# Flamingo layers on one core: the second pass's attention output by two levels of seven block products

## The chip, the cores and the metric

The kernel runs on one core of a Trainium2 chip. The metric is device time in microseconds (us) of one execution; the time before is the median of three runs. The program is static: every engine (TensorE, VectorE, ScalarE, GpSimd, and SyncE, which issues nearly all transfers) executes its own list of instructions in order, and semaphores tie the lists together. A profile of one execution lies beside the times.

## The reference

Two layers act on x, 8 sequences of 256 rows of 1024 numbers in float32. Layer 0 adds a gated autocorrelation attention (FFT, top 11 lags, softmax) and a gated linear layer with low-rank parts. Layer 1, which the change concerns, adds gated cross attention over a context and a gated linear layer:

```
x = x + tanh(g_xattn[0]) * autocorrelation(layernorm(x), ctx)
x = x + tanh(g_ffn[0])   * (W h + b + one of four low-rank parts)
q = rope(h @ wq)   # 32 heads of 128; k = rope(ctx @ wk), v = ctx @ wv: 8 heads each
w = softmax(where(mask, q k^T / sqrt(128), -1e9))
x = x + tanh(g_xattn[1]) * (concat_heads(w v) @ wo)       # wo: 4096 x 1024
x = x + tanh(g_ffn[1])   * (W1' h + b1)                   # fourier part folded into W1'
```

h is the layernorm of x at that point. All products are in float32.

## The kernel before, in words

Rows go through in two passes (p = 0, 1) of four sequences, eight tiles of 128 rows each. A pass has four stages: autocorrelation with the keys and values of the pass beside it (keys_values), lora_ffn, attention, fourier_ffn. Keys and values go to DRAM and come back by head group.

Large matrix products are done as seven block products in place of eight. Of A B with both cut into 2 x 2 blocks, left_operands makes four combinations of A's blocks, right_operands four of B's, and the results of the products 1, 2, 6, 7, 4, 5, 3 (SEVEN) are combined by combine (L220, into a fresh tile) or add_product (L252, straight into x, scaled by the gate): partial sums named u and w are carried along. Combinations of weights are made once, stored in DRAM, and loaded in later blocks (load_wq L862, load_wo L884).

Attention has 16 steps a pass: two blocks of 512 rows times eight head groups. In a step, for each of four combinations (n: sequence, l: head half) the program issues scores (L969: four products, a memset by GpSimd, a masked copy and a maximum by VectorE, exp by ScalarE, two scalings by VectorE), then some of the next step's queries, then values of the combination before (L1006: transposes, ScalarE copies, products). The output products of the step before fill in between: outputs (L942), seven products by two row tiles, each of two matmuls of 128x512 into one PSUM bank. The lists q_fill and o_fill (L1046) say how many products are issued in each quarter; the last step's outputs come after the loop (L1089). Queries take seven products of eight matmuls of 128x256 (L929), and rope (L714) turns them: three VectorE products and one GpSimd add (L723). PSUM tiles of queries and outputs share four banks (ps_mm).

A scheduler puts the instructions of each engine in order when the program is built: it goes by program order as priority, takes what it holds ready first, and inserts semaphore waits and buffer reuse. So a transfer or a GpSimd operation that is ready early may stand well ahead of its place in the program. Buffers are pools with a number of slots per tag: weights of queries and outputs have seven slots of 512 KB each, and a load waits until TensorE has released its slot. All transfers but the scattered output rows are issued by SyncE in one list.

## Time and profile before

| | us |
|---|---|
| median of three runs | 3401.23 (3399.96 to 3401.61) |
| profiled execution | 3396.83 |
| its span, first to last instruction | 3395.0 |
| TensorE busy in the span | 3314.1 |
| VectorE | 2252.4 |
| GpSimd | 1354.6 |
| ScalarE | 859.7 |
| one attention step, in either pass | 65.65 |

Times in the table are of one profiled execution but for the first line. A row of the profile's groups reads: line of the kernel, engine, operation, tiles written and read, shapes, count, then busy time and mean nanoseconds of one, then the time the engine sat idle just ahead of them and what ended it. Matmuls overlap, so that the mean of one is longer than the distance between two.

### The profile page before, as it was taken

The page shows a single profiled execution, that of the slowest core. Times are in us where ns is not written, and L with a number is a line of the kernel's source. Part 1 is how long each engine was busy: PE and PEld are TensorE (multiplying, and loading weights), DVE is VectorE, ACT ScalarE, POOL GpSimd, SP SyncE. Part 2 cuts the span into 40 slices and gives each one's busy share as a digit, 9 for nine tenths or more (in the row PEclk, how much of TensorE's full clock was granted, in tenths as well). Part 3 has the DMA queues.
Part 4 walks back from the last instruction along what each step waited for, and adds up shares of the span by engine and source line. Part 5 has one row for each costly group of instructions (what it writes and reads, how often), then busy time and mean ns, then how long its engine had stood idle before and what let it go on. Part 6 is the DMA issues. An engine that isn't in the chain of part 4 may idle for free. (4 is left out here: it accounts for less than half of the span.)

```text
span 3395.0 us, 36926 instructions
## 1 busy us (share of the span) xinstructions
PE 3314.1 (98%) x12784; PEld 2279.1 (67%) x12784; DVE 2252.4 (66%) x4229; ACT 859.7 (25%) x2061; POOL 1354.6 (40%) x1213
## 2 busy tenths in 40 slices
PE   8899999999999999999999999999999999999999
PEld 6566546767767776775467766577767776776654
DVE  7787666877777666665657775556666666666563
ACT  1233111322222222222123321112222322222220
POOL 4665212344443443344335542123443444344332
PEclk9999999999999999999999999999999999999999
DMA  7433634333333333343153424053333333333411
GB/s 270 170 115 102 207 115 155 130 140 127 137 127 131 121 119 123 118 155 118 56 196 130 147 96 146 17 173 115 118 125 120 115 118 121 121 118 122 158 44 50
DMA packets 161864, 431.72 MB, mean 127 GB/s; under 512 B 21476, under 2 KB 56292, under 8 KB 161678
## 3 DMA queue, kind: packets, MB, share of 16 engines
q1 hardware_dynamic: 160526, 425.17, 36.3%
q0 software_dynamic: 1152, 4.19, 0.3%
q8 instruction: 102, 1.67, 0.2%
q14 instruction: 84, 0.69, 0.1%
HBM read 350.66 MB, written 78.64 MB: 126 GB/s over the span
## 5 line engine op out<-in xcount | busy, mean ns | idle before, releaser
L723 POOL TENSOR_TENSOR qT<-rope,rope 128x512 f32<-128x512 f32 x128 | 170.2, 1330 | 867.5 <-DVE rope L722 867.5
L958 PE MATMUL po<-wo,oT 128*128 128x512 f32 x960 | 432.1, 593 | 0.0
L929 PE MATMUL ps_q<-xn,wq 128*128 128x256 f32 x1920 | 428.9, 379 | 0.0
L375 DVE SCALAR_TENSOR_TENSOR x<-po,tg,x 128x512 f32<-128x512 f32 x376 | 269.1, 745 | 196.0 <-PE po L958 70.5
L929 PEld LDWEIGHTS ps_q<-xn,wq 128*128 128x128 f32 x1920 | 364.8, 190 | 50.5 <-PE po L682 0.5
L991 ACT ACTIVATE s<-s,nmx 128x256 f32<-128x256 f32 x512 | 256.0, 501 | 277.0 <-DVE nmx L988 276.5
L986 DVE COPY_PREDICATED s<-keep,ps_s 128x512 f32<-128x512 uint8 x256 | 185.9, 729 | 182.2 <-PE ps_s L977 177.7
L958 PEld LDWEIGHTS po<-wo,oT 128*128 128x128 f32 x960 | 177.4, 190 | 175.6 <-issue 170.5
L958 PE MATMUL po<-wo,oS 128*128 128x512 f32 x640 | 287.7, 592 | 0.3 <-DVE x L375 0.3
L929 PE MATMUL ps_q<-xn_t,wq 128*128 128x256 f32 x1280 | 285.6, 379 | 0.0
L1018 ACT COPY wT<-pt 128x512 f32<-128x512 f32 x256 | 138.1, 590 | 515.9 <-PE pt L1012 515.7
L929 PEld LDWEIGHTS ps_q<-xn_t,wq 128*128 128x128 f32 x1280 | 243.2, 190 | 33.1
L1023 PE MATMUL av<-wT,v 128*128 128x256 f32 x1024 | 246.2, 383 | 5.1 <-ACT wT L1018 5.1
L977 PE MATMUL ps_s<-kT,qT 128*128 128x256 f32 x1024 | 247.9, 379 | 0.0
L1023 PEld LDWEIGHTS av<-wT,v 128*128 128x128 f32 x1024 | 191.4, 190 | 80.0 <-issue 44.0
L1000 DVE TENSOR_SCALAR s<-s,tot 128x256 f32<-128x256 f32 x512 | 220.0, 470 | 7.7
L985 POOL MEMSET s<- 128x512 f32 x256 | 130.0, 527 | 220.7 <-PE pt L1012 219.0
L958 PEld LDWEIGHTS po<-wo,oS 128*128 128x128 f32 x640 | 118.9, 190 | 136.7 <-issue 128.9
L977 PEld LDWEIGHTS ps_s<-kT,qT 128*128 128x128 f32 x1024 | 191.6, 190 | 25.3 <-DVE x L375 0.5
L258 POOL TENSOR_TENSOR x<-x,part 128x512 f32<-128x512 f32 x80 | 109.1, 1364 | 229.5 <-ACT part L257 222.1
L988 DVE TENSOR_REDUCE nmx<-s 128x2 f32<-128x512 f32 x256 | 175.0, 685 | 8.3
L263 POOL TENSOR_TENSOR x<-x,part 128x512 f32<-128x512 f32 x80 | 104.7, 1310 | 172.7 <-DVE part L375 157.0
(257 smaller groups left out, 5594.0 us busy)
## 6 DMA issues: line engine op xcount, KB each, us to landing
wq<-in_wq_dram SPq DMA_DIRECT2D x104, 512.0 KB, 3.2
wo<-in_wo_dram SPq DMA_DIRECT2D x104, 512.0 KB, 3.2
wq<-wq_d SPq DMA_DIRECT2D x96, 512.0 KB, 3.2
wo<-wo_d SPq DMA_DIRECT2D x96, 512.0 KB, 3.2
w<-w_d SPq DMA_DIRECT2D x36, 512.0 KB, 4.8
wk<-in_wk_dram SPq DMA_DIRECT2D x26, 512.0 KB, 5.9
wv<-in_wv_dram SPq DMA_DIRECT2D x26, 512.0 KB, 3.8
wk<-wk_d SPq DMA_DIRECT2D x24, 512.0 KB, 4.5
```

The source lines that it names most:

```text
L375: nc.vector.scalar_tensor_tensor(xs, ps, g, xs, ALU.mult, ALU.add)
L723: nc.gpsimd.tensor_add(dst, t0, t1)
L929: nc.tensor.matmul(ps[:, l, :], wops[r][:, l, c, :], xo[r][:, c, :], start=(c == 0), stop=(c == KH - 1),)
L958: nc.tensor.matmul(po, ops[r][:, h, t * P : (t + 1) * P], wops[r][:, h, :], start=(h == 0), stop=(h == 1),)
L977: nc.tensor.matmul(ps[:, t, :], qT[i, n][:, l, t * P : (t + 1) * P], kT[:, n * S : (n + 1) * S], start=True, stop=True,)
L985: nc.gpsimd.memset(s, MASKED)
L986: nc.vector.copy_predicated(s, keep[b], ps)
L988: nc.vector.tensor_reduce(nmx, s, AX.X, ALU.max, negate=True)
L991: nc.scalar.activation(s[:, t, :], s[:, t, :], AF.Exp, bias=nmx[:, t : t + 1], accum_out=tot[:, t : t + 1],)
L1000: nc.vector.tensor_scalar(s[:, t, :], s[:, t, :], tot[:, t : t + 1], None, ALU.mult)
L1018: nc.scalar.copy(wT[i], pt)
L1023: nc.tensor.matmul(av[:, i, :], kv[step][1][:, n * 2 + c, :], wT[i][:, c, :], start=(c == 0), stop=(c == 1),)
```

## The change

In pass 2 (the last), outputs gives way to outputs_of_two. It waits for the attention outputs of two head groups (two steps) and treats the product of 512 rows, 1024 columns of heads and 1024 output columns as seven products of halves, each of which is again seven products of halves: 49 products, each of two matmuls of 128x256. The left operands of the first level are made in place by GpSimd, those of the second level by GpSimd a product ahead (finer); the second level's results are gathered in c from u, v and m, the first level's in x by further adds. The right operands (49 per pair of groups) are read from wo2_d, 256 KB each, two per transfer (stream_wo). They are made in pass 1 by finer_weights: 28 chunks, each with two loads, four GpSimd subtractions and seven stores, issued one per quarter from the second block on. Fill lists of pass 2 count single products. Outputs of a pair spread over the two steps that follow it; the last pair's come after the loop.

To make room, rope works in place with one temporary, keys and queries are combined straight into the tile that is stored or used, key and value loads have three buffers for four, attention outputs 13 for 8 in pass 2, and the keys' rope table is loaded in each pass into a tile of the first stage.

```diff
--- before.py
+++ after.py
...
-    tab = const.tile([P, 2, S], F32, name="tab")
     tab_q = const.tile([P, 2, S], F32, name="tab_q")
...
+    wo2_d = [dram.tile([P, 49, 2, S], F32, name=f"wo2_d{i}") for i in range(N_KV // 2)]
...
-    def rope(dst, ps, cos, sin, pool):
+    def rope(x, cos, sin, pool):
         H = P // 2
-        t0 = pool.tile([P, 2, S], F32, tag="rope0", name="rope0", bufs=1)
-        t1 = pool.tile([P, 2, S], F32, tag="rope1", name="rope1", bufs=1)
+        t = pool.tile([P, 2, S], F32, tag="rope", name="rope", bufs=1)
         tab = lambda t: t.unsqueeze(1).to_broadcast([t.shape[0], 2, S])
-        nc.vector.tensor_mul(t0, ps, tab(cos))
-        nc.vector.tensor_mul(t1[0:H], ps[H:P], tab(sin[H:P, :]))
-        nc.vector.tensor_mul(t1[H:P], ps[0:H], tab(sin[0:H, :]))
-        nc.gpsimd.tensor_add(dst, t0, t1)
-
-    def keys_values(n, groups, pools):
+        nc.vector.tensor_mul(t[0:H], x[H:P], tab(sin[H:P, :]))
+        nc.vector.tensor_mul(t[H:P], x[0:H], tab(sin[0:H, :]))
+        nc.vector.tensor_mul(x, x, tab(cos))
+        nc.gpsimd.tensor_add(x, x, t)
+    def keys_values(n, groups, pools, tab):
...
-                dest = (lambda: new("c")) if kind == "wk" else out_tile
-                done = combine(r, ps, tiles, new, dest)
+                done = combine(r, ps, tiles, new, out_tile)
...
-                        kT = out_tile()
-                        rope(kT, c, tab[:, 0, :], tab[:, 1, :], w1)
+                        rope(c, tab[:, 0, :], tab[:, 1, :], w1)
                         place = kT_d.rearrange("(q l i) p t -> q i p l t", l=2, i=2)
                         nc.sync.dma_start(
-                            place[i_u, i, :, :, t0 + j * S : t0 + (j + 1) * S], kT
+                            place[i_u, i, :, :, t0 + j * S : t0 + (j + 1) * S], c
...
-            xn = pool.tile([P, D], F32, tag="xn", name="xl")
+            xn = new()
...
+            def finer_weights():
+                for two in range(N_KV // 2):
+                    for n, r in enumerate(SEVEN):
+                        w = [
+                            w1.tile([P, 2, HALF], F32, tag=f"fine{k}", name=f"fine{k}")
+                            for k in range(2)
+                        ]
+                        for k in range(2):
+                            nc.sync.dma_start(w[k], wo_operand(two * 2 + k, r))
+                        q = [[w[k][:, :, j * S : (j + 1) * S] for j in range(2)] for k in range(2)]
+                        t = [
+                            w1.tile([P, 2, S], F32, tag=f"fine_t{i}", name=f"fine_t{i}")
+                            for i in (1, 2, 4)
+                        ]
+                        ops = right_operands(nc.gpsimd, q, *t)
+                        for i, r2 in enumerate(SEVEN):
+                            nc.sync.dma_start(wo2_d[two][:, n * 7 + i], ops[r2])
+                        yield
+            def stream_wo():
+                places = [
+                    wo2_d[g // 2][:, n : min(n + 2, 49)]
+                    for blk, g in steps[::2]
+                    for n in range(0, 49, 2)
+                ]
+                tiles = []
+                for n in range(len(places)):
+                    while len(tiles) < min(n + 6, len(places)):
+                        src = places[len(tiles)]
+                        tiles.append(big_tile(go, [2, 2, S], "wo"))
+                        nc.sync.dma_start(tiles[-1][:, 0 : src.shape[1]], src)
+                    for i in range(places[n].shape[1]):
+                        yield tiles[n][:, i]
...
-                kT = w2.tile([P, NB], F32, tag="kv", name="kT", bufs=4)
+                kT = w2.tile([P, NB], F32, tag="kv", name="kT", bufs=3)
-                v = w2.tile([P, NBT, DH], F32, tag="kv", name="v", bufs=4)
+                v = w2.tile([P, NBT, DH], F32, tag="kv", name="v", bufs=3)
...
-                    done = combine(r, ps, tiles, lambda tag: half(tag, 1), lambda: half("c", 2))
+                    done = combine(r, ps, tiles, lambda tag: half(tag, 1), lambda: half("qT", 7))
                     if done:
-                        qT[done[1]] = half("qT", 8)
-                        rope(qT[done[1]], done[0], tab_q[:, 0, :], tab_q[:, 1, :], w1)
+                        qT[done[1]] = done[0]
+                        rope(done[0], tab_q[:, 0, :], tab_q[:, 1, :], w1)
...
+            def outputs_of_two(blk, qs):
+                g, ng = tg_x[1], ntg_x[1]
...
+                s1 = [half("oT", 13) for _ in qs]
+                for q, s in zip(qs, s1):
+                    nc.gpsimd.tensor_add(s, q[1][0], q[1][1])
+                    nc.gpsimd.tensor_sub(q[1][0], q[0][0], q[1][0])
+                at = lambda i, k: [q[i][k] for q in qs]
+                ops = {1: at(0, 0), 2: at(0, 1), 6: at(0, 0), 7: at(1, 0), 4: at(1, 1), 5: s1}
+                ops[3] = ops[2]
...
+                def finer(r):
+                    q = [[o[:, :, t * P : (t + 1) * P] for o in ops[r]] for t in range(2)]
+                    made = {1: q[0][0], 2: q[0][1], 4: q[1][1]}
+                    def make():
+                        for i, (op, y, z) in {
+                            5: (nc.gpsimd.tensor_add, q[1][0], q[1][1]),
+                            7: (nc.gpsimd.tensor_sub, q[0][0], q[1][0]),
+                            6: (nc.gpsimd.tensor_sub, 5, q[0][0]),
+                            3: (nc.gpsimd.tensor_sub, q[0][1], 6),
+                        }.items():
+                            made[i] = w2.tile([P, 2, P], F32, tag="oI", name=f"oI{i}", bufs=5)
+                            op(made[i], *(made[v] if isinstance(v, int) else v for v in (y, z)))
+                            yield
+                    return made, make()
+                left, make = finer(SEVEN[0])
+                for _ in make:
+                    pass
+                part = None
+                for n, r in enumerate(SEVEN):
+                    g1, g2 = (ng, g) if r == 4 else (g, ng)
+                    c = [half("co", 6) for t in range(2)]
+                    for r2 in SEVEN:
+                        w = next(wo_stream)
+                        po = ps_mm.tile([P, S], F32, tag="mm", name="po")
+                        for h in range(2):
+                            nc.tensor.matmul(
+                                po, left[r2][:, h, :], w[:, h, :], start=(h == 0), stop=(h == 1)
+                            )
+                        scaled = nc.vector.scalar_tensor_tensor
+                        if r2 == 1:
+                            u = quarter("o_u", 1)
+                            nc.scalar.activation(u, po, AF.Copy, scale=g1)
+                        elif r2 == 2:
+                            scaled(c[0][:, 0, :], po, g1, u, ALU.mult, ALU.add)
+                        elif r2 == 6:
+                            scaled(u, po, g1, u, ALU.mult, ALU.add)
+                        elif r2 == 7:
+                            v = quarter("o_w", 1)
+                            scaled(v, po, g1, u, ALU.mult, ALU.add)
+                        elif r2 == 4:
+                            scaled(c[1][:, 0, :], po, g2, v, ALU.mult, ALU.add)
+                        elif r2 == 5:
+                            m = quarter("o_m", 1)
+                            nc.scalar.activation(m, po, AF.Copy, scale=g1)
+                            nc.gpsimd.tensor_add(u, u, m)
+                            nc.gpsimd.tensor_add(c[1][:, 1, :], v, m)
+                        elif r2 == 3:
+                            scaled(c[0][:, 1, :], po, g1, u, ALU.mult, ALU.add)
+                        if r2 in (2, 6, 7, 5):
+                            next(coming[1], None)
+                        if r2 != 3:
+                            yield
+                    for t in range(2):
+                        ct = c[t].rearrange("p b s -> p (b s)")
+                        add = lambda eng, y: eng.tensor_add(y, y, ct)
+                        if r == 1:
+                            add(nc.gpsimd, x[t][0][0])
+                        elif r == 2:
+                            add(nc.vector, x[t][0][0])
+                        elif r == 6:
+                            add(nc.vector, part[t])
+                            nc.gpsimd.tensor_add(x[t][0][1], x[t][0][1], part[t])
+                        elif r == 7:
+                            nc.vector.tensor_add(ct, ct, part[t])
+                            add(nc.gpsimd, x[t][1][0])
+                            add(nc.gpsimd, x[t][1][1])
+                        elif r == 4:
+                            add(nc.vector, x[t][1][0])
+                        elif r == 5:
+                            add(nc.vector, x[t][0][1])
+                            add(nc.vector, x[t][1][1])
+                        elif r == 3:
+                            add(nc.vector, x[t][0][1])
+                    if r == 1:
+                        part = [y.rearrange("p b s -> p (b s)") for y in c]
+                        for q, s in zip(qs, s1):
+                            nc.gpsimd.tensor_sub(q[0][0], s, q[0][0])
+                    elif r == 2:
+                        for q in qs:
+                            nc.gpsimd.tensor_sub(q[0][1], q[0][1], q[0][0])
+                    left = coming[0]
...
-                oT[n][l] = half("oT", 8)
+                oT[n][l] = half("oT", 13 if paired else 8)
...
+            paired = p == NPASS - 1
+            nothing = iter(())
+            fine = finer_weights() if p == 0 else nothing
+            if paired:
+                new_xl = lambda: big_tile(go, [D], "xl")
+                wo_stream = stream_wo()
+            else:
+                new_xl = lambda: w1.tile([P, D], F32, tag="fine0", name="xl")
...
-            last, before, nothing = None, None, iter(())
-
-            q_fill = {0: (2, 2, 1, 1), len(steps) - 1: (0, 0, 0, 0)}
-            o_fill = {len(steps) - 1: (2, 2, 2, 1)}
+            last, before, o_gen = [], None, nothing
+            end = len(steps) - 1
+            if paired:
+                q_fill = {0: (2, 2, 1, 1), 1: (2, 2, 2, 1), end: (0, 0, 0, 0)}
+                o_fill = {k: (0, 5, 10, 10) if k % 2 == 0 else (3, 5, 8, 8) for k in range(end)}
+                o_fill[end] = (6, 6, 6, 6)
+            else:
+                q_fill = {0: (2, 2, 1, 1), end: (0, 0, 0, 0)}
+                o_fill = {k: (0, 1, 3, 3) for k in range(end)}
+                o_fill[end] = (2, 2, 2, 1)
+            middle = 4 if paired else 1
...
+            def start_outputs():
+                if paired:
+                    got = outputs_of_two(last[0][0][0], [oT for _, oT in last])
+                else:
+                    s = [half(f"oS{j}", 1) for j in (1, 2, 4)]
+                    got = outputs(last[0][0], left_operands(nc.gpsimd, last[0][1], *s))
+                last.clear()
+                return got
...
-                o_gen = nothing
                 for i, (n, l) in enumerate(((0, 0), (0, 1), (1, 0), (1, 1))):
                     got = scores(step, l, n, qT)
                     nq = q_fill.get(k, (3, 3, 1, 0))[i]
-                    no = o_fill.get(k, (0, 1, 3, 3))[i]
+                    no = o_fill[k][i]
                     fill_from(q_gen, nq)
+                    mid = min(no, middle)
                     if i > 0:
-                        fill_from(o_gen, no - 1)
+                        fill_from(o_gen, no - mid)
                     if before is not None:
-                        values(*before, lambda: fill_from(o_gen, 1 if no else 0))
+                        values(*before, lambda: fill_from(o_gen, mid))
                     before = step, l, n, got, oT
-                    if i == 0 and k > 0:
-                        s = [half(f"oS{j}", 1) for j in (1, 2, 4)]
-                        o_gen = outputs(last[0], left_operands(nc.gpsimd, last[1], *s))
-                        fill_from(o_gen, no)
+                    if i == 0:
...
-                    if i == 0:
+                    if i == 0 and not paired:
                         load_wo(step)
-                for gen in (q_gen, o_gen):
-                    for _ in gen:
+                    if step[0] > 0:
+                        next(fine, None)
+                for _ in q_gen:
+                    pass
+                if not paired or k % 2:
+                    for _ in o_gen:
                         pass
-                last = step, oT
+                last.append((step, oT))
                 oT = [[None, None], [None, None]]
...
-            s = [half(f"oS{j}", 1) for j in (1, 2, 4)]
-            for _ in outputs(last[0], left_operands(nc.gpsimd, last[1], *s)):
+            for _ in start_outputs():
                 pass
...
+            tab = kw1.tile([P, 2, S], F32, name="tab")
...
+            nc.sync.dma_start(tab, a["rope"])
```

## Prediction

> **What bounds the kernel now.** I read the page first (span, engines, slices), then the windows of single steps, then the order of TensorE at the stage's end, then the queue's waits and the DMA rows. The page says who is full:
>
> ```profile
> span 3395.0 us, 36926 instructions
> PE 3314.1 (98%) x12784; PEld 2279.1 (67%) x12784; DVE 2252.4 (66%) x4229; ACT 859.7 (25%) x2061; POOL 1354.6 (40%) x1213
> L958 PE MATMUL po<-wo,oT 128*128 128x512 f32 x960 | 432.1, 593 | 0.0
> L929 PE MATMUL ps_q<-xn,wq 128*128 128x256 f32 x1920 | 428.9, 379 | 0.0
> ```
>
> TensorE has 2% idle, and none ahead of the attention's products. One step (a block of 512 rows, a head group) repeats every 65.65 us; two of them, the first in pass 1, the second in pass 2 (columns: length; PE, PEld, DVE, ACT, POOL busy; clock, DMA share, GB/s):
>
> ```profile
> 1161.65:1227.30 65.65, 65.65 (x265) 47.31 (x265) 42.71 (x78) 20.47 (x51) 26.51 (x26) 1.00 0.35 121
> 2293.00:2358.65 65.65, 65.65 (x266) 47.31 (x265) 41.72 (x73) 17.72 (x48) 27.48 (x27) 1.00 0.36 121
> ```
>
> TensorE is busy for the whole step; the others have room: VectorE 64%, GpSimd 42%, DMA 36%. So a microsecond of product removed there is a microsecond of span, until another engine or a wait takes over. At the end of pass 2's attention the last step's outputs stand alone (TensorE's timeline: start, length):
>
> ```profile
> 3268.58 7.03 PE L958 MATMUL po<-wo,oT 128*128 128x512 f32 x16
> 3275.45 7.03 PE L958 MATMUL po<-wo,oS 128*128 128x512 f32 x16
> 3284.77 2.85 PE L370 MATMUL pt<-ident,xn 128*128 128x128 f32 x16 [2.29 <-DVE xn L360]
> ```
>
> In the waits of the DMA queue, SP mostly stands waiting for TensorE to free a weight buffer, so it has slack now; the DMA rows (KB, us to landing) and a GpSimd row give prices:
>
> ```profile
> SPq L881 <- PE ps_q L929: 665.9, 161, 8.6
> wq<-wq_d SPq DMA_DIRECT2D x96, 512.0 KB, 3.2
> kT_d<-k SPq DMA_DIRECT2D x32, 256.0 KB, 2.5
> 27.00:30.00 3.00, 2.57 (x12) 1.96 (x11) 2.96 (x7) 1.22 (x2) 0.40 (x1) 1.00 1.03 420
> 1804.00:1807.20 3.20, 3.20 (x15) 2.59 (x14) 3.09 (x15) 1.58 (x3) 0.70 (x1) 1.00 0.23 82
> L296 POOL TENSOR_TENSOR co<-co,mf 128x320 f32<-128x320 f32 x3 | 2.6, 864 | 1.3 <-DVE mf L295 1.3
> ```
>
> **What the Trainium skill says.** "DMA: Bandwidth & Descriptors", section "Anatomy of one DMA", fits about 2.0 us plus bytes over 436 GB/s, most of the 2 us being the receipt; that page's fit is for another issuing path, yet the rows above agree: 3.2 us for 512 KB (fit 3.2), 2.5 for 256 KB (fit 2.6). "HBM Reference", its opening specifications, gives about 425 GB/s for a core streaming alone; the trace's best 3 us moved 420, and nothing here shows that rate held for hundreds of microseconds. "GPSIMD Engine Reference", section 3.1 (elementwise cycle accounting), says two-input elementwise work costs GpSimd about 2.6 cycles an element; the trace has 1.27 us for 128x512 and 0.864 for 128x320, 2.1 ns an element, so 0.73 us for 128x256.
>
> **Part 1, products of pass 2.** Before: 7 products x 2 tiles x 2 halves = 28 matmuls a step, two instructions each, 8 in 3.44 us: 56 x 0.43 = 24.1, 48.2 a pair of steps. After: 49 products x 2 matmuls x 2 instructions of 128x256. Queries run this shape at 16 in 3.45 us, 0.216 each, with weight loads of 190 ns beneath: 196 x 0.216 = 42.3. Saved 5.86 a pair, and eight pairs give -46.9 us.
>
> **Part 2, their evacuation.** No row has these shapes from PSUM; I bound VectorE's 128x256 by half of 745 ns (0.37) and the 128x256 rows of 0.47, and take 0.45. A pair: 35 x 0.45 + 14 adds of 0.69 = 25.4 us against 28 x 0.745 = 20.9 before; VectorE goes from 42 to about 44 of a 62.7 us step. ScalarE: 14 copies of about 0.5, it is at 27%. GpSimd: 28 operand sums and 14 combines at 0.73, and 16 operations of 128x512 (four opening sums, four in-place differences, eight output adds) at 1.27: 30.7 + 20.3 = 51 us a pair against 24 x 1.27 = 31 before; with memsets, ropes and the queries' combines, 37 of 62.7 a step. All under TensorE's product on average. But u, w and m have one buffer, PSUM four banks, now 0.86 us each and no longer 1.72: a late engine shows after 3.4 us instead of 6.9. Bounds 0 and 25 us over the steady steps; I take 5. If VectorE is late, the queries' evacuation, ropes and the next scores queue behind it. Step 1 has no outputs to fill with (pairs start at step 2): like step 0, +2 (0 to 5). Step 15 has only 24 products: VectorE 33 of 38 us: +3 (0 to 6). The last pair now stands alone: TensorE 42.3 us, but GpSimd's 51 for it is longer, so +8 (0 to 12). Sum of these waits +18.
>
> **Part 3, finer weights, in pass 1.** 28 chunks, each two loads of 512 KB, four GpSimd subtractions (4 x 1.27 = 5.1 us) and seven stores of 256 KB: 2.88 MB, 80.7 MB in all. In the built order they begin near the end of step 6 and stand five to a step, so 13.13 us each at the present pace. They are on no one's path only while this holds: GpSimd executes in order, and behind a subtraction that waits for its load stand the memset (L985) that the scores need and the rope's add (L723). GpSimd itself: 26.5 + 25.4 = 52 of 65.65. DMA: 121 GB/s x 65.65 = 7.94 MB, plus 14.4: 22.4 MB a step. The rate lies between 420 (large loads) and 356 (0.262 MB in 0.23 x 3.2 us of share, the kT_d store of 1 KB runs): at 370, 60.5 us. The chain of one chunk has single buffers: loads wait for the last chunk's stores, stores for the sums. By hand, with the end of a chunk's last sum as zero, a store costing 0.745 us of transfer and a 512 KB load 1.4, 0.9 us before and 0.9 after the transfer (3.2 = 1.4 + 1.8), transfers one after another: two stores issued during the last sum are through at 1.2; the three issued after it at 2.0, 2.7 and 3.5, the last landed at 4.4. A weight load is through at 4.9, the next chunk's first load, which only waited for earlier stores, at 6.3. Its second load waits for the store landed at 4.4 and is issued at 4.5; through at 7.7, landed at 8.6. The first sum is done by then; three more, 1.27 each and a start of 0.1, end at 12.5. In this cycle the transfers idle some 1.6 us while the sums run. So a step needs 60.5 + 5 x 1.6 = 68.5 us, +2.9; over 28/5 = 5.6 steps +16. Some 8 us are covered, since scores stand a quarter step (16 us) ahead of the values that use them and the softmax between needs half: +8. Bounds: 0 (rate of 400 and more), and +44 if GpSimd's own bursts are added in each step. In the built order two memsets and two combines stand inside one chunk (2 x 0.53 + 2 x 1.27 = 3.6 us), about ten microseconds of output adds, memsets and a rope ahead of another, where 8.7 are free (+1.3), and left operands with what follows ahead of a third (11.2 against 8.7, +2.5). Five chunks of 12.5, these 7.4 and in most chunks one more weight load in the way (0.9 x 5 = 4.5) make 74.4, about 75: 9.4 x 5.6 - 8 = 44. I stay nearer the low end, because such a burst and a backlog of transfers overlap. SP is passed by 252 more issues of about 0.36 us; each weight load behind them has a step's slack.
>
> **Part 4, the rest.** Turning in place keeps three VectorE products and one GpSimd add per quarter and removes no instruction. Keys' combines now write the tile that the store reads, so VectorE (its products of the correlation behind it) may wait for a store of 2.5 us that formerly only GpSimd awaited: -1 to +6, I take +1. Keys' and values' buffers go from 4 to 3, and queries' from 8 plus 2 to 7: cover is the half step between a load and its use; zero, a few us if SP is late in pass 1. The keys' rope table is loaded in each pass instead of once: 0 to 2 us, I take none, as only the second pass's row loads queue behind it.
>
> Sum: -46.9 + 18 + 8 + 1 = -20. The profiled execution took 3396.8 (span 3395.0 and 1.8 around it), so 3377; the median of the runs is 4.4 above it, so **3381 us**.
>
> **Rivals.** *Chunks set pass 1's pace (slower).* Place: steps 7 to 12 of pass 1. For it: transfers would go from 36% to over 90% of their rate, with single buffers and an in-order GpSimd at 80%. Against: the chain by hand is 12.5 us of 13.13. It decides from 14.4 us a chunk: 28 x 1.3 - 8 = 28 = the rest's gain. At 75 us a step: 3401 - 47 + 19 + 44 = 3417.
> *Evacuation eats the gain (same).* 34 us over 392 products is 0.09 us each; for it VectorE at 80% in quarters with ten products, against it zero waits in the attention now at 64%: about 3401.
> *All hidden.* Chunks fit, steady steps don't wait: -46.9 + 8 + 2 = -37: 3364.
> That 128x256 products don't cost half is excluded by L929's pace.
>
> **Chances.** Forecast (3364 to 3394) 0.37, all hidden 0.13, eaten 0.14, chunks or worse 0.36. A measurement here tells about 0.2%, 7 us, from no change. Faster 0.50, same 0.14, slower 0.36. Range 3358 to 3434: below it 0.08 (the last pair hidden too), above it 0.12 (chunks at 75 us and 25 us of evacuation together); the forecast's own 3364 to 3394.
>
> **What would show it.** Right: pass 2's pairs 125 to 127 us with TensorE full; a last pair of about 50 us with waits on GpSimd; pass 1's steps 7 to 12 at 66 to 69 us. Wrong: TensorE waiting there for the softmax or ropes, GpSimd idle ahead of right_operands' subtractions on a fine load, steps above 72 us; or in pass 2 waits of po on VectorE in every pair.

## The result, and the profile after

The changed kernel takes 3502.97 us (median of four runs, 3501.9 to 3506.25), the kernel before 3400.89 us beside it: a ratio of 1.0302 (95% interval 1.0284 to 1.032), 102 us slower, where 3381 was predicted and 3434 was the top of the range. The profiled execution took 3506.25 us. The page, with the rows that answer to those shown of before:

```profile
span 3504.5 us, 40018 instructions
PE 3312.0 (95%) x13456; PEld 2426.1 (69%) x13456; DVE 2359.1 (67%) x4397; ACT 888.5 (25%) x2141; POOL 1692.6 (48%) x1597
```

TensorE's busy time is what it was, though its products became fewer: a slower granted clock (last section) and modelled ends that stretch over short waits fill the difference. So I counted the products instead. In all that follows a stage runs from the first query product to the first transposition after the last values product; "product" is the sum over the stage's matmuls of 0.2148 us per 256 columns (the undisturbed distance), "lost" the rest. All of it is worked out from the starts of TensorE's instructions, in us ("lost" so holds waits and products that ran slowly):

| | before | after | difference |
|---|---|---|---|
| up to pass 1's attention | 562.7 | 557.8 | -4.9 |
| pass 1's attention | 1063.1 | 1133.0 | +69.9 |
| from there to pass 2's attention | 600.6 | 606.4 | +5.8 |
| pass 2's attention | 1058.4 | 1097.1 | +38.7 |
| of it product / lost | 1048.2 / 10.2 | 1000.1 / 97.0 | -48.1 / +86.8 |
| end | 110.3 | 110.2 | -0.1 |

The spans differ by 109.5 us, the medians by 102: the profiled execution is 3.3 us above the median of its runs, that of the kernel before 4.1 below. The saving is there, 48.1 us (46 with each shape's own distance, 0.216 us for 128x256 and 0.429 for 128x512). Two new losses stand against it: 70 us in pass 1, and 87 in pass 2. The windows show where, first two steps of pass 1 with chunks of finer weights in them (columns: length; PE, PEld, DVE, ACT, POOL busy; clock, DMA share, GB/s):

```profile
1135.60:1210.30 74.70, 67.91 (x265) 47.77 (x264) 54.59 (x84) 20.47 (x51) 50.75 (x46) 0.95 0.84 288
1210.30:1287.40 77.10, 68.64 (x265) 48.82 (x264) 51.48 (x72) 17.93 (x48) 52.38 (x47) 0.93 0.89 299
```

Steps 7 to 12 take 462.3 us together, 77 each, against six times 65.65. Now two steps of pass 2, the later one of a pair and the first of the next, 132.7 us where 125.4 would be free of waits:

```profile
2509.40:2572.00 62.60, 60.41 (x294) 52.46 (x294) 44.32 (x81) 19.07 (x52) 31.14 (x37) 1.00 0.48 156
2572.00:2642.10 70.10, 66.39 (x322) 57.80 (x321) 45.70 (x84) 20.07 (x54) 46.33 (x51) 1.00 0.51 165
```

TensorE's largest waits over the whole span are two that the kernel before has not (what waited, for what: us in total, times, longest):

```profile
PE po L996 <- DVE qT L245: 40.9, 6, 13.4
PE po L1059 <- DVE co L1067: 33.3, 20, 4.2
```

Both name VectorE, which is busy 67% of the span. So the question is what VectorE itself stood on. Its waits and GpSimd's from 1050 to 1480 us, most of steps 7 to 12:

```profile
DVE rope L720 <- POOL qT L241: 53.8, 6, 17.5
DVE s L1134 <- POOL s L1133: 42.7, 10, 11.1
POOL fine_t L215 <- DMA fine<-wo_d: 55.6, 12, 7.4
POOL fine_t L215 <- DMA fine<-in_wo_dram: 39.5, 7, 8.4
```

The chain is GpSimd on a fine load (95 us), VectorE on GpSimd, TensorE on VectorE. Its first link is in part direct and for the rest a backlog: in the 99 us in which VectorE stood on GpSimd, GpSimd itself stood on a load for 20, ran subtractions for 36 and other operations for 44. One place of it in the three engines' order of time (start, length, operation, idle time ahead in brackets):

```profile
1448.75 1.26 POOL L215 TENSOR_TENSOR fine_t<-fine 128x512 f32<-128x512 f32 x1 [5.93 <-DMA fine<-in_wo_dram]
1451.65 1.26 POOL L241 TENSOR_TENSOR qT<-w,m 128x512 f32<-128x512 f32 x1
1452.95 0.69 DVE L720 TENSOR_TENSOR rope<-qT,tab_q 64x512 f32<-64x512 f32 x1 [17.51 <-POOL qT L241]
1462.61 0.68 DVE L245 TENSOR_TENSOR qT<-ps_q,u 128x512 f32<-128x512 f32 x1
1448.02 1.88 PE L996 MATMUL po<-wo,oS 128*128 128x512 f32 x4
1463.35 3.78 PE L996 MATMUL po<-wo,oS 128*128 128x512 f32 x4 [13.45 <-DVE qT L245]
```

The queries' combine L241 stands behind the subtraction; VectorE's rope product waits 17.5 us for it, its softmax work and the emptying of a query bank (L245) stand behind that, and TensorE has no bank. In pass 2 (2440 to 3340 us), VectorE's largest wait is of the same kind, but for GpSimd's own queue, and one place of it stands a little ahead of those two steps:

```profile
DVE co L1081 <- POOL o_u L1078: 69.4, 20, 7.5
```

```profile
2457.24 1.25 POOL L1113 TENSOR_TENSOR oT<-oT 128x512 f32<-128x512 f32 x1
2459.14 0.71 POOL L1078 TENSOR_TENSOR o_u<-o_u,o_m 128x256 f32<-128x256 f32 x1
2459.88 0.48 DVE L1081 SCALAR_TENSOR_TENSOR co<-po,tg,o_u 128x256 f32<-128x256 f32 x1 [7.52 <-POOL o_u L1078]
2464.79 0.47 DVE L1067 SCALAR_TENSOR_TENSOR co<-po,tg,o_u 128x256 f32<-128x256 f32 x1
2465.32 3.68 PE L1059 MATMUL po<-wo,oI 128*128 128x256 f32 x8 [2.90 <-DVE co L1067]
```

ScalarE had written m by 2453.3. The add that needs it (L1078) came 5.8 us later, behind a turn, three operand terms, two memsets and an in-place difference. VectorE stood for 7.5 us in that gap, the longest of the 20 waits (3.5 us on average). Five operations of its own then stood ahead of L1067, and four banks of 0.86 us do not last so long.

### The profile page after: what moved, and what is told of

It is laid out like the page before. It is cut to its first block, busy times and chain, and to the rows that moved or that the text cites. A ratio compares the mean times of both kernels' runs of the same rounds, so it can differ in the third digit from the quotient of the medians.

```text
span 3504.5 us, 40018 instructions
## 1 busy us (share of the span) xinstructions
PE 3312.0 (95%) x13456; PEld 2426.1 (69%) x13456; DVE 2359.1 (67%) x4397; ACT 888.5 (25%) x2141; POOL 1692.6 (48%) x1597
## 5 line engine op out<-in xcount | busy, mean ns | idle before, releaser
L723 POOL TENSOR_TENSOR qT<-qT,rope 128x512 f32<-128x512 f32 x128 | 171.9, 1343 | 535.7 <-DVE qT L722 535.7
L1059 PE MATMUL po<-wo,oI 128*128 128x256 f32 x896 | 231.5, 398 | 47.0 <-DVE co L1067 33.3
L376 DVE SCALAR_TENSOR_TENSOR x<-po,tg,x 128x512 f32<-128x512 f32 x248 | 177.8, 743 | 128.1 <-PE po L683 42.5
L1148 DVE TENSOR_SCALAR s<-s,tot 128x256 f32<-128x256 f32 x512 | 253.8, 536 | 7.2
L1059 PEld LDWEIGHTS po<-wo,oI 128*128 128x128 f32 x896 | 172.4, 198 | 85.6 <-DVE co L1067 41.7
L996 PE MATMUL po<-wo,oT 128*128 128x512 f32 x448 | 202.2, 594 | 3.5 <-DVE w L235 3.5
L720 DVE TENSOR_TENSOR rope<-qT,tab_q 64x512 f32<-64x512 f32 x128 | 98.0, 766 | 147.8 <-POOL qT L241 139.6
L259 POOL TENSOR_TENSOR x<-x,part 128x512 f32<-128x512 f32 x48 | 65.4, 1363 | 220.3 <-ACT part L258 220.3
L1059 PE MATMUL po<-wo,oT 128*128 128x256 f32 x672 | 169.7, 384 | 0.0
```

What stands on the lines that cost most here:

```text
L376: nc.vector.scalar_tensor_tensor(xs, ps, g, xs, ALU.mult, ALU.add)
L723: nc.gpsimd.tensor_add(x, x, t)
L996: nc.tensor.matmul(po, ops[r][:, h, t * P : (t + 1) * P], wops[r][:, h, :], start=(h == 0), stop=(h == 1),)
L1059: nc.tensor.matmul(po, left[r2][:, h, :], w[:, h, :], start=(h == 0), stop=(h == 1))
L1148: nc.vector.tensor_scalar(s[:, t, :], s[:, t, :], tot[:, t : t + 1], None, ALU.mult)
```

## The experiments

Stages in us, as in the table above; every kernel's ratio is to the kernel before in the same session. The stages are those of one profiled execution each. Where pass 1 is that of the changed kernel (e4, e6, e11) its attention took 1130.0 to 1136.5 us, and where pass 2 is (e1, e2, e3, e10) 1093.6 to 1098.1: differences within that spread are not read.

| | pass 1's attention | pass 2's attention | median | ratio (95%) |
|---|---|---|---|---|
| e1, no subtractions | 1070.4 | 1096.6 | 3443.06 | 1.012 (1.0102 to 1.0138) |
| e2, no loads | 1077.1 | 1093.6 | 3454.97 | 1.0151 (1.0134 to 1.0168) |
| e3, loads ahead | 1099.5 | 1097.1 | 3467.28 | 1.0182 (1.0165 to 1.0199) |
| e4, adds on VectorE | 1136.5 | 1058.2 | 3467.87 | 1.0184 (1.0166 to 1.0201) |
| e5, turn in place alone | 1062.9 | 1058.6 | 3398.0 | 0.9989 (0.9983 to 0.9996) |
| e6, operands later | 1130.0 | 1099.9 | 3503.77 | 1.0307 (1.0287 to 1.0328) |
| e7, single subtractions, adds | 1076.1 | 1054.6 | 3412.28 | 1.0036 (1.0023 to 1.0048) |
| e8, and two sums | 1081.4 | 1036.7 | 3394.53 | 0.9978 (0.997 to 0.9987) |
| e9, done by step 14 | 1074.4 | 1038.1 | 3383.11 | 0.9963 (0.9949 to 0.9977) |
| e10, four a step | 1080.1 | 1098.1 | 3450.91 | 1.0146 (1.0126 to 1.0165) |
| e11, two sums alone | 1134.4 | 1091.0 | 3498.25 | 1.0293 (1.0277 to 1.0308) |

### Pass 1: transfers, GpSimd's time, or its waiting

**e1.**

```diff
-                        ops = right_operands(nc.gpsimd, q, *t)
+                        ops = [q[0][0], q[1][0], q[1][1], q[0][1]]
                         for i, r2 in enumerate(SEVEN):
-                            nc.sync.dma_start(wo2_d[two][:, n * 7 + i], ops[r2])
+                            nc.sync.dma_start(wo2_d[two][:, n * 7 + i], ops[i % 4])
```

> Left out: the four GpSimd subtractions of each chunk of finer weights in pass 1; the loads and stores stay (same number and size, the stores take the loaded tiles). So the finer weights are wrong, and with them pass 2's outputs. Theory W (in steps 7 to 12 GpSimd stands in its queue on the fine loads, and the memsets and ropes behind them come late): steps 7 to 12 of pass 1 return from about 77 us to 66 to 67 us, and the whole to about 3435 us (3425 to 3445). Rival R (the transfers alone are too many: weights late or the DMA rate at its end): the steps stay at 74 us or more, the whole at 3490 or more. Rival G (GpSimd's own 5.1 us a chunk): as W; the next run tells these two apart. Pass 2's attention unchanged at about 1097 us for all three.

One step of it, from the windows:

```profile
1128.50:1194.10 65.60, 65.60 (x265) 47.28 (x264) 46.20 (x85) 20.47 (x51) 26.35 (x27) 1.00 0.93 310
```

With every transfer kept, at 310 GB/s and 93% of the engines' time, TensorE is full and the step is back to 65.6 us. Rival R falls: the traffic alone costs nothing here. Pass 1's attention is 7 us over before, of which two steps of the first block have 4.9.

**e2.** Here `pin` is the framework's keep_in_program_order: the instruction stays behind all that the program has issued on its engine before it.

```diff
+                w = [w1.tile([P, 2, HALF], F32, tag=f"fine{k}", name=f"fine{k}") for k in range(2)]
+                for k in range(2):
+                    nc.sync.dma_start(w[k], wo_operand(k, 1))
                 for two in range(N_KV // 2):
                     for n, r in enumerate(SEVEN):
...
-                            nc.sync.dma_start(wo2_d[two][:, n * 7 + i], ops[r2])
+                            nc.sync.dma_start(wo2_d[two][:, n * 7 + i], ops[1 + i % 3])
...
-        eng.tensor_sub(t1, q[0][1], q[0][0])
+        pin(eng.tensor_sub(t1, q[0][1], q[0][0]))
```

> Left out: all fine loads but the first two (the subtractions work on one pair of tiles again and again, the stores, as many and as large, take tiles that no subtraction writes), and each chunk's first subtraction is kept at its place in the order of the program, one chunk a quarter step in steps 8 to 14. The finer weights are wrong, and so are pass 2's outputs. Theory W (waiting for loads is what delays): with nothing to wait for the steps are 65.7 to 67 us, the whole about 3435 (3425 to 3445), though GpSimd computes as much as before. Rival G (GpSimd's own time): four chunks of 5.1 us a step still delay memsets and ropes: steps 70 us or more, the whole 3460 or more. Rival R (traffic): half of it is gone, steps between 66 and 70.

Steps with four chunks take 66.6 to 67.0 us: theory W's edge, and inside rival R's 66 to 70, which e1 rules out. At this place and pace GpSimd's own time is worth up to 1.35 us a step (67.0 less 65.65), not the 11.4 lost; it does have a share, and the whole came out 10 us above W's range.

**e10.** The one line `pin` of e2 in the changed kernel, loads and all.

> The changed kernel with one thing altered: each chunk's first subtraction is kept at its place in the order of the program, which gives four chunks a step in steps 8 to 14 (16.4 us each) and not five in steps 7 to 12 (13.1 us). Theory C (a chunk's own chain of loads, subtractions and stores takes 15.9 us, as it did on average in the changed kernel, and the excess over its share of a step is what pass 1 loses): 16.4 us leave it half a microsecond, so pass 1's attention takes 1070 to 1090 us, the whole 3440 to 3465. Rival H (any load directly at the head of GpSimd's queue delays, whatever the pace): pass 1 stays above 1110 us, the whole above 3480.

```profile
1203.00:1270.00 67.00, 65.95 (x265) 47.22 (x264) 51.28 (x72) 17.71 (x48) 46.63 (x42) 1.00 0.85 291
POOL fine_t L215 <- DMA fine<-wo_d: 18.8, 4, 5.1
POOL fine_t L215 <- DMA fine<-in_wo_dram: 10.8, 2, 5.9
```

(The first line is of the windows, the other two of GpSimd's waits.) The full work, at four chunks a step and not five, costs the same 67.0 us as without loads; only around the last chunk, whose first subtraction stands 7.9 us on its load, a step takes 62.9 us where it took 55.1. In 400 us of the steps the waits on fine loads come to 30 us (95 in 430 us of the changed kernel). H falls, and the times are where C put them.

But C's reason, a chain of 15.9 us that 16.4 leave room for, is not shown. Keeping the subtraction in place altered three things at once. The pace is one. The second is SyncE's order: the second load of the next chunk is issued 2.7 us after a chunk's last subtraction on average, about 6 in the changed kernel. Seven of e10's chunks did start as soon as their load had landed, 9.6 to 11.3 us (once 14.1) after the chunk before: there a chunk's own chain is mostly shorter than the 13.1 us of five a step. The third is the place in GpSimd's order: VectorE stands on GpSimd for 44 us in 430, not 99, and in them subtractions run for 6 us, not 36. No run tells the three apart. The order of the changed kernel came from the scheduler, which put the subtractions where it held them ready: the first starts at 1020.6 us, in step 6, and the program issues it in step 8.

**e3.**

```diff
+                        yield
                         ops = right_operands(nc.gpsimd, q, *t, tc.keep_in_program_order)
...
-                    if step[0] > 0:
+                    if k > 1:
                         next(fine, None)
```

> Nothing left out: each chunk is cut in two, the loads a quarter step ahead of the subtractions, the chunks begin in step 2 and not in step 8, so some two a step over steps 2 to 15 instead of five over steps 7 to 12, and each first subtraction is kept at its place in the order of the program. Theory W: steps of pass 1 66 to 68 us throughout, pass 1's attention at most 20 us above the 1063 us of the kernel before, the whole 3435 to 3455. Rival R: as W, since the traffic is spread too. Rival G: the same 143 us of GpSimd stand in the order, spread over 14 steps, so half of the 70 us is left: 3465 or more.

A miss for W, and the whole, 3467.28 us, is where rival G had it: 36 of the 70 us are left. But they are not spread as G's would be. With some two chunks a step the steps of the second block are free after the first of them (67.2), while those of the first, 2 to 5, take 73 to 75 us. A step of each:

```profile
869.80:943.20 73.40, 68.12 (x266) 48.16 (x265) 57.28 (x79) 17.83 (x48) 38.00 (x35) 0.98 0.57 201
1287.80:1353.40 65.60, 65.60 (x265) 47.31 (x264) 46.44 (x72) 17.83 (x48) 36.61 (x34) 1.00 0.64 209
```

GpSimd and transfers are alike, and GpSimd waits for no fine load there. VectorE, which makes weight sums in the first block, is 11 us fuller. That bursts of 5.1 us on GpSimd cost more where VectorE has less room fits; no run isolates it. So a step can lose 8 us without GpSimd waiting for any load.

### Pass 2: who is late in the evacuation

**e4.**

```diff
-                            nc.gpsimd.tensor_add(u, u, m)
-                            nc.gpsimd.tensor_add(c[1][:, 1, :], v, m)
+                            nc.vector.tensor_add(u, u, m)
+                            nc.vector.tensor_add(c[1][:, 1, :], v, m)
```

> Nothing left out: the two additions of m in each block of pass 2's outputs (L1078, L1079) move from GpSimd to VectorE. Theory P (TensorE's 87 us of loss in pass 2's attention come from VectorE standing in its queue on GpSimd's o_u, which stands behind operand sums, memsets and turns): the waits for it (69 us on VectorE) go, pass 2's attention falls from 1097 to about 1050 (1035 to 1065), the whole to about 3455. Rival V (VectorE itself is the late engine, and 28 additions a pair, some 11 us, make it later): pass 2 stays at 1095 to 1110, the whole at 3500 to 3515. Rival Q (four PSUM banks of 0.86 us each are too few for any evacuation): between, 3480 to 3500.

VectorE got 14 more operations a pair (two in each of seven blocks; the 28 of the expectation is a miscount), and pass 2's attention became 39 us shorter. The wait that replaces the 69 us (VectorE's waits):

```profile
DVE o_u L1078 <- ACT o_m L1077: 13.4, 16, 0.9
```

Theory P holds; V, that VectorE's amount of work is the limit, falls, and so does Q. The edit also takes some 10 us a pair (14 x 0.71) from GpSimd, and no run separates that from the place of the two adds.

**e6 and e11.** The first edit is e6, the others are e11.

```diff
-                        if r2 in (2, 6, 7, 5):
+                        if r2 in (6, 7, 4, 3):
...
-                    c = [half("co", 6) for t in range(2)]
+                    c = [half("co", 5) for t in range(2)]
-                            u = quarter("o_u", 1)
+                            u = quarter("o_u", 2)
-                            m = quarter("o_m", 1)
+                            m = quarter("o_m", 2)
```

> Nothing left out: in pass 2 the four finer operands of the next block are made one or two products later (after products 6, 7, 4, 3 of the block and not after 2, 6, 7, 5), so that their buffers have been read by then. Theory Q (GpSimd's 141 us of waits for TensorE to free an operand's buffer hold up o_u, queued behind): pass 2's attention falls from 1097 to 1070 us or less, the whole to 3475 or less. Rival T (o_u is late by the other work in GpSimd's queue: turns, memsets, whole adds): pass 2 stays at 1090 us or more, the whole at 3495 to 3505.

> The changed kernel with two buffers each for o_u and o_m and five for co in pass 2, the additions still on GpSimd. Theory P (VectorE stands in its queue on GpSimd's additions, whatever the buffers): pass 2's attention 1085 us or more, the whole at 3490 or more. Rival S (the single buffers are what ties the blocks together): 1065 us or less, the whole at 3472 or less.

Neither wait for operand buffers (Q) nor single sums (S) is the cause while the adds stand on GpSimd: +3 us and -6 us in pass 2's attention, little more than the spread between executions.

**e7 and e8.** e7 is e4 and e6 together with finer_weights rewritten: single subtractions, each pinned, and the next chunk's loads issued after the last one, two places ahead of its first; the last edit stands twice in each quarter. e8 adds e11's buffers.

```diff
+                    for r2, op, y, z in (
+                        (5, t[0], q[0][1], q[0][0]),
+                        (7, q[0][1], q[1][1], q[0][1]),
+                        (6, t[1], q[1][1], t[0]),
+                        (4, t[2], t[1], q[1][0]),
+                    ):
+                        pin(nc.gpsimd.tensor_sub(op, y, z))
+                        store(r2, op)
+                        if r2 != 4:
+                            yield
+                    if c + 1 < len(chunks):
+                        w = load(*chunks[c + 1])
+                    for _ in range(2):
+                        yield
...
+                    if k >= 7:
+                        fill_from(fine, 2)
```

> Nothing left out: pass 1's subtractions one at a time from step 7 on, some three chunks a step, the next chunk's loads well ahead of its first subtraction; in pass 2 the additions of m on VectorE and the operands made later. Theory W: with no wait on loads at the head of GpSimd's queue and no burst over 1.3 us, pass 1's attention takes 1063 to 1075 us (1133 in the changed kernel). Rival G (GpSimd's time): 1077 us or more, as without loads. Pass 2: theory P 1045 to 1055 us; if the late operands are neutral 1058, as with the additions alone. The whole 3385 to 3400.

> As the run before it, and two buffers each for o_u and o_m, with five for co. Theory S (ScalarE's opening product of a block waits until VectorE has read the last block's o_u, up to 5 us, while TensorE fills its four banks): pass 2's attention falls by another 10 us or more, to 1035 to 1045, the whole 3375 to 3390. Rival V (VectorE's own queue is what is late): no change against the run before it, within 3 us.

In pass 2 both came as theories P and S have it: 1054.6, then 1036.7 us. So the single sums do bind, but only once GpSimd's adds no longer stand ahead of them: -18 us here, -6 alone. Pass 1 missed, and the whole with it in both runs. In e7 its steps are at 65.6 us but for step 7 (67.7) and the last but one (57.2 for 55.1), though GpSimd still stands on fine loads for 34 us in steps 8 to 14, up to 5.8 at once: a wait of that kind need not cost anything. Of the 13 us over before, some 7 are lost at the end, where chunks were left over; in e8 some 12 of 18. The orders of GpSimd and TensorE there, in e8:

```profile
1594.19 1.26 POOL L941 TENSOR_TENSOR fine<-fine,fine 128x512 f32<-128x512 f32 x1 [4.08 <-DMA fine<-in_wo_dram]
1602.95 2.08 PE L1193 MATMUL av<-wT,v 128*128 128x256 f32 x4 [6.61 <-ACT wT L1188]
```

The last scores' memsets stood behind that subtraction.

**e9.** A denser pace (`2 + i % 2` in one of the two places), so that no chunk is left for step 15.

> As the run with two sums, but the single subtractions a little denser (18 places a step and not 16), so that the last chunk ends in step 14 and none stands ahead of step 15's values. Theory W: in that run pass 1's attention took 1081 us and not 1063 because two fine loads stood at the head of GpSimd's queue at its end, ahead of the memsets of the last scores (6.8 us of TensorE's time at one place): now 1064 to 1071, the whole 3375 to 3385. Rival G (GpSimd's own time in the steps): pass 1 stays at 1076 us or more, the whole at 3388 or more.

The 6.6 us wait is gone, but the denser steps take up to 68.3 us, so pass 1's attention is 1074.4 us, 3 us above theory W's range and below rival G's. This kernel beats the changed one and, by 0.4%, the one before: 3383.11 us against 3397.26 beside it, a ratio of 0.9963.

### The fourth part alone

**e5.** The rope, keys_values, buffer and table edits of the change's diff, on the kernel before.

> On the kernel before, only the change's fourth part: turning in place, keys' combines straight into the stored tile, three buffers for keys and values, seven for queries, the keys' table loaded in each pass. Theory (this part costs about nothing: in the changed kernel the stage before pass 1's attention is 4.9 us shorter, and the stages between the two attentions 5.8 us longer): within 5 us of before, about 3402 (3396 to 3409). Rival (one buffer for the turn's table products and the in-place products keep VectorE waiting for GpSimd, and that fed the losses in both attentions): 3415 or more.

3398.0 us against 3401.59: a gain of 0.1%, and both attentions as before. Where the gain lies is not shown: the profiled execution was the fastest of the 20 (3387.33 us). Nor do the stages between the attentions show where the changed kernel's +5.8 us come from. They took 596.9 us here and 600.6 before, but 601.9 to 608.4 in e1 to e4 and e6 to e11, where they are the same as in the changed kernel, so that part of the 5.8 is the execution's. The rest stays open.

## Why the prediction was wrong

**Part 1 was right:** -46.9 predicted, -48.1 counted (-46 with each shape's own distance).

**Part 2 failed at "I take 5" for the steady steps, and in its bounds of 0 to 25.** The pairs take 133 to 146 us, not 125 to 127; steps 2 to 14 lose 75 us, 6 before, and the whole stage 87 more than before where 18 stood. The step compared each engine's amount of work with the step's length. Those amounts were about right (VectorE 44 and 46 us in the two windows, 44 predicted; GpSimd 31 and 46, 37 predicted), and no engine was full. What it left out is order: a block's results go from TensorE through ScalarE, GpSimd and VectorE, each in order, so the add of 0.7 us is as late as what stands ahead of it in GpSimd's queue. e4 shows it by moving two adds: -39 us with VectorE busier. Second buffers for the sums gave 18 more once that was done (e8); of the 37 us then still lost, 10 stood before. "A late engine shows after 3.4 us" was the right yardstick, and VectorE's waits for the add were up to 7.5 us; I priced it as a rare case. The remark that opening terms, memsets, turns and output adds share GpSimd's queue was made for pass 1 only. The figure for step 1 (+2, 0 to 5) held: two waits on ScalarE's copies cost 2.8 us there. The last pair was to lose 8 us (0 to 12) and lost 14.8, beyond its bound.

**Part 3 failed at "+8", in the chain of 12.5 us a chunk.** First subtractions start at:

```profile
L215 POOL TENSOR_TENSOR fine_t<-fine x28: 1257/1268/3317, 1020.6 to 1448.8; 128x512 f32<-128x512 f32 x28
```

That is 428.2 us for 27 intervals, 15.86 each. In the chain by hand a chunk's first subtraction starts 7.3 us after the last one of the chunk before, and the four take 5.2; measured were 8.5 and 7.3 us. The chain's durations were those of quiet transfers, 3.2 us for 512 KB and 2.5 for 256 KB. In the loaded steps (rows of issues: KB, median us to landing):

```profile
fine<-wo_d SPq DMA_DIRECT2D x32, 512.0 KB, 5.2
wo_d<-fine SPq DMA_DIRECT2D x112, 256.0 KB, 3.9
```

These landings, 2.0 and 1.4 us longer, can account for the first part, which grew by 1.2 us. The second grew by 2.1, on GpSimd: 1.1 us of other operations between a chunk's subtractions and 0.9 of standing, mostly for the second load. Such operations were seen, but went into the bound of 44 and not into the 8.

The rest of the step's formula then gives 28 x (15.86 - 13.13) - 8 = 68 us; steps 7 to 12 lost 68.4. That is no second proof: the intervals lie in the lengthened steps and so contain the loss, and that the 8, an estimate, fits so well is luck. The rival's threshold, 14.4 us a chunk, lies below what was measured, as the rival needs; no run tests it by itself, since e10 altered more than the pace. So it is shown that the term was 70 us and not 8, that the transfers alone cost nothing (e1: the word "rate" in that step was beside the point), and that one subtraction of four kept in its place gives back 53 us (e10). How much of that is pace, how much place and how much SyncE's order stays open.

**Part 4** was +1, with bounds -1 to +6; alone it gives -3.6 us (e5), below its bounds.

**The chances** put chunks at 75 us a step (+44) and evacuation at 25 as the two far ends and hardly let them come together. The measured terms were 70 and 87. Both rivals were named with the right place, and both were priced from averages. The cause named for the second, VectorE's amount of work, is not the one that e4 shows.

What would show it: pairs above 127 us, steps above 72 us, TensorE waiting in each pair on VectorE, GpSimd idle ahead of right_operands' subtractions on a fine load: these signs listed as "wrong" all came. In pass 1, though, TensorE waited for a query bank that VectorE emptied late (40.9 us), and not for the softmax or the ropes themselves.

## What to carry to other kernels

Here work added to an engine with idle time cost the lateness it gave to what was queued behind it, not its amount: look at what stands behind an operation that waits for a transfer or for another engine, and give it its own pace and place. A chain through transfers is to be priced with the landing times of the loaded stage, and with the other work that its engine does in between. A scheduler that issues such work as soon as it holds it ready can bunch it: keeping it at its place in the program gave back 53 of 70 us here. A small add between two engines of an evacuation was better on one of them, even though that one was the busier.

## What the runs showed of the hardware

**A wait costs TensorE more than itself.** The four products at 1463.35 above took 3.78 us after a wait of 13.45, the same four 1.88 ahead of it; the eight at 2465.32 took 3.68 after 2.90 us, against 1.89 undisturbed. The Trainium skill, "TensorE: Matmul & The Clock Gate", Part 1, has half the clock after an idle window of about 3.4 us and for about 3.4 us of work; here 2.9 us of idle time sufficed. It did not always: the first line is the stretch after that wait, the second the one after another wait of 2.90 us (PEclk is the third figure from the end).

```profile
2465.40:2468.80 3.40, 3.40 (x8) 2.60 (x9) 3.37 (x10) 1.57 (x5) 1.30 (x2) 0.50 0.14 27
2599.40:2602.30 2.90, 2.86 (x16) 2.33 (x17) 2.87 (x9) 1.76 (x8) 1.58 (x3) 1.00 0.25 47
```

In the kernel before, the clock was full throughout both attentions; in the changed kernel it was half for 51 us of pass 1's and 41 of pass 2's. At half the clock up to half of such a stretch is lost, so an estimate of up to 26 and 21 us of the two losses is slow products and not waiting. The mean granted clock was 0.980 after, 0.992 before.

**GpSimd's adds hold VectorE up.** Two pairs of the same scaling, 2.3 us apart, the first while GpSimd adds (its operations at 1456.39 to 1461.8), the second after it:

```profile
1459.80 2.17 DVE L1148 TENSOR_SCALAR s<-s,tot 128x256 f32<-128x256 f32 x2
1462.08 0.62 DVE L1148 TENSOR_SCALAR s<-s,tot 128x256 f32<-128x256 f32 x2
```

Over the changed kernel one takes 1.08 us on average where GpSimd's adds cover at least 80% of it (108 of them), 0.35 where they cover under 5% (377); masked copies and maxima show no such difference (0.73 and 0.69 us either way). The Trainium skill, "SBUF — State Buffer", section "SBUF: two separate sides", says that the two engines share a pair of ports which an instruction of one of them (of VectorE's, not of every kind) holds to its end; these figures agree. The prediction, which gave each engine its own time, did not use it. No run separates what it adds to the losses.
